# A gated recurrence over 512 steps: one VectorE transpose cut in two and two VectorE instructions moved to other places of the step

## The chip, the cores and the metric

The kernel runs on one core of one Trainium2 chip. The metric is the time of one execution in device microseconds. Three runs of the kernel before gave 1627.81, 1628.59 and 1628.85 us, a median of 1628.59 us.

## What is computed

The input `x` has 8 sequences of 512 steps with 512 features. A recurrent cell runs over the steps, and its states are added to `x`.

```
def step(h, x_t):                                   # h: 8 x 512, x_t: 8 x 512
    fused = sigmoid(concat([x_t, h]) @ w_W + w_b)   # 8 x 1024
    hidden_state, output_state = split(fused, 2)    # r and z below
    memory_state = x_t @ wx_W + wx_b + hidden_state * (h @ wh_W + wh_b)
    h_new = output_state * h + (1 - output_state) * tanh(memory_state)
    return h_new, h_new
_, hs = scan(step, cond_1024, x over its steps)
result = x + hs
```

The products with `x_t` can be made ahead of time. The products with `h` can't: each step needs the state of the step before, in all 512 features.

## The kernel before

**Layout.** The 512 state features are cut into four chunks of 128. Chunks 0 and 1 are half A (`hf` = 0 in the code), chunks 2 and 3 are half B (`hf` = 1). A state tile `hT` holds 128 features on the partitions and the 8 sequences beside each other, for 4 steps; 8 such tiles are used in turn. Four column groups of TensorE (32 columns each) work side by side, so one product with a chunk of the state is four matmuls, and float32 makes two passes of each.

**TensorE, one step.** The string `ORDER` sets the order: A0 to A3, then D0 to D3, then H2 and H3. The letter is the PSUM bank that is added to, the digit is the chunk of the state that is the stationary operand. Bank A collects half A's inner product, z and r (and half B's part of the inner product from chunks 0 and 1), bank D half B's z and r, and bank H the rest of half B's inner product. A0 and A1 stream 256 columns, A2 and A3 192, D0 to D3 128, H2 and H3 64. Behind them come products for later `x`, which do not depend on the state (bank `xp`): three blocks of 96 columns in a step, four in one step of sixteen, none in the last steps.

**VectorE, one step.** Its program is in the order in which the Python code is written. Half A comes first: transposes out of bank A (`turn_r`, `turn_h(0)`, `turn_z`), two scans `memory(0, q)`, a transpose for half B out of bank A (`turn_part`), the transpose of half B's r out of bank D (`turn_r_b`), then the update scans. `memory(hf, q)` is a scan that forms the argument of the tanh for chunk `q` of a half (tile `m`); ScalarE takes the tanh and writes it into `hT`. `update(hf, q)` is a scan that forms the new state of that chunk from z (`hd0A` or `hd0B`), the tanh and the old state. `turn_h(1)` transposes half B's inner product ("hh") from bank H into `md1B`. `turn_sz` transposes half B's z, on which ScalarE has taken the sigmoid already (tile `sz`), into `hd0B`, in two pieces of 32 columns, one for each chunk.

**Waits inside VectorE.** A scan that reads what an earlier VectorE instruction wrote needs a wait on that instruction's end. The kernel puts a memset of one column of `idle` in front of the scan, and the memset carries the wait (`settle`, and the memset at the end of `turn_sz`). The second piece of z has no such memset of its own; `update(1, 1)` waits for it itself.

**Who waits for whom.** On TensorE the weight loads of A0, A1, A2 and A3 each wait for one of the four updates of the step before, in the order `update(0, 0)`, `update(0, 1)`, `update(1, 0)`, `update(1, 1)`. On ScalarE the order is: sigmoid of half A's r and z, tanh of half A's chunks, sigmoid of half B's r in two pieces (`md0B`), sigmoid of half B's z (`sz`), tanh of half B's chunks, two copies of the new state. Behind the updates VectorE does work that has no hurry: it adds up the `x` products (`drain`, L431), turns them for later steps (`turn_x`, L319), and in the first steps forms differences of weights (`inner_weight`, L338). GpSimd adds `x` to the state and works on later `x`.

**Lines.** L219 is every matmul, L285 every ScalarE function, L565 every scan, L592 `turn_h`, L600 and L632 the memsets that wait, L629 z's transposes.

Of the kernel before, what the change touches and what calls it, by code (L numbers as in the profile page):

```python
# [24 lines left out]
SYNC = mybir.DependencyInfo(mybir.DependencyClass.Sync, mybir.DependencyReason.DATA)  # L25
# [51 lines left out]
def tile_cond_rnn_residual(  # L77
# [38 lines left out]
    nc = tc.nc  # L116
# [29 lines left out]
    def x_of(c, k, t, n):  # L146

        e, t = divmod(t, TC // 2)
        if c == 0 and e == 0:
            first = head[:, 512 : 512 + NX].rearrange("p (k n) -> p k n", k=NQ)  # L150
            return first[:, k, t * B : (t + n) * B]
        return xins[c][:, e, k, t * B : (t + n) * B]
# [18 lines left out]
    def pair(n, name, rows, slots):  # L171

        return const.tile([P, 2, rows, slots], F32, name=name).rearrange("p c n s -> p n c s")
# [3 lines left out]
    NH = 2 * GS  # L177
# [4 lines left out]
    md1 = [[pair(n, f"md1{n}{i}", 32, m) for i in range(2)] for n, m in (("A", 2), ("B", 3))]  # L182
    hd0 = [[pair(n, f"hd0{n}{i}", m, 3) for i in range(2)] for n, m in (("A", B), ("B", 32))]
# [24 lines left out]
    def state(hf, i, slot=2):  # L208

        s = i % GS  # L210
        return hT[hf][i % NH][:, B * s : B * s + B, :, slot]
# [72 lines left out]
    def act(key, out_, in_, func, **kw):  # L284
        inst = nc.scalar.activation(out_, in_, func, **kw).ins  # L285
        if key in written:
            tc.declare_no_dep(inst, written[key], reason="ordered through VectorE")
        written[key] = inst
        return inst

    def seed(g):

        at = COLS if g else slice(0, 512)
        nc.scalar.copy(bank_of(g)[:, at], bias[:, at])
# [228 lines left out]
    pool_done = {}  # L523
    for i in range(T):
        g, s = divmod(i, GS)
        c, t = divmod(i, TC)
# [36 lines left out]
        def scan(c_, out_, d0, d1):  # L563

            return nc.vector.tensor_tensor_scan(  # L565
                *[t_[:, :, c_].rearrange("p n c s -> p (n c s)") for t_ in (out_, d0, d1)],
                0.0,
                ALU.mult,
                ALU.add,
            ).ins  # L570

        pa = ps["A"][:, HU:] if i else xps[0][:, :HALF]
        raw = {"h": (pa[:, :HU], ps["H"]), "z": (pa[:, HU : 2 * HU],), "r": (pa[:, 2 * HU :], ps["D"][:, HU:])}
# [6 lines left out]
        h_done = [None, None]  # L580
# [8 lines left out]
            )  # L589

        def turn_h(hf):
            inst = nc.vector.transpose(  # L592
                md1[hf][g % 2][:, :, :, hf].rearrange("p n c -> p c n"), raw["h"][hf]
            ).ins
            h_done[hf] = inst
            if hf == 0 and i + 1 - NH in pool_done:
                tc.add_manual_dep(inst, pool_done[i + 1 - NH].name, SYNC)

        def settle(hf):
            inst = nc.vector.memset(idle[:, IDLE - 2 + hf : IDLE - 1 + hf], 0.0).ins  # L600
            tc.add_manual_dep(inst, h_done[hf].name, SYNC)
# [12 lines left out]
        def turn_r_b():  # L614
            t_, _ = turned("r", 1)
            for q in range(2):
                act(
                    ("r", 1, q, g % 2, s),
                    md0[1][g % 2][:, rows, q : q + 1, 2].rearrange("p n c -> p c n"),
                    t_[:, q : q + 1],  # L620
                    AF.Sigmoid,
                )
            sz = work.tile([P, HU], F32, tag="sz", name=f"sz_{i}")
            act(("sz", i % 4), sz, ps["D"][:, :HU], AF.Sigmoid, scale=-1.0)
            return sz

        def turn_sz(sz):
            done = [
                nc.vector.transpose(hd0[1][i % 2][:, :, q, 2], sz[:, 32 * q : 32 * q + 32]).ins  # L629
                for q in range(2)  # L630
            ]
            mark = nc.vector.memset(idle[:, IDLE - 3 : IDLE - 2], 0.0).ins  # L632
            tc.add_manual_dep(mark, done[0].name, SYNC)

        def turn_part():
            nc.vector.transpose(md1[1][g % 2][:, :, :, 0].rearrange("p n c -> p c n"), ps["A"][:, :HU])  # L636
# [6 lines left out]
        def memory(hf, q):  # L643

            c_ = slice(q, q + 1)
            scan(c_, ms[hf], md0[hf][g % 2][:, rows], md1[hf][g % 2][:, rows])
            act(("n", hf, q, i % NH), state(hf, i, 1)[:, :, c_], ms[hf][:, :, c_, 1 + hf], AF.Tanh)

        def update(hf, q):
            new = hT[hf][(i + 1) % NH][:, B * s1 : B * s1 + B]  # L650
            z_ = hd0[hf][i % 2][:, rows] if hf else hd0[hf][i % 2]
            return scan(slice(q, q + 1), new, z_, hT[hf][i % NH][:, rows])

        turn_r()
        turn_h(0)
        turn_z()
        memory(0, 0)
# [6 lines left out]
        sz = turn_r_b()  # L664
        update(0, 0)
        turn_h(1)
        update(0, 1)
        settle(1)
        if i == 0:

            seed(6)
        memory(1, 0)
        if i == T - 1:
            nc.gpsimd.tensor_tensor(
                ot[:, t, :2, :].rearrange("p c n -> p n c"),
                x_of(c, slice(0, 2), t, 1).rearrange("p c n -> p n c"),
                state(0, T),
                ALU.add,
            )
        memory(1, 1)  # L680
        turn_sz(sz)
        update(1, 0)
        update(1, 1)
        for hf in range(2):
            act(("h", hf, (i + 1) % NH), state(hf, i + 1, 0), state(hf, i + 1), AF.Copy)
# [129 lines left out]
```

## Time and profile before

| what | before |
|---|---|
| median of 3 runs | 1628.59 us (1627.81 to 1628.85) |
| profiled execution, first to last instruction | 1625.9 us |
| TensorE matmul busy | 1616.3 us (99%) |
| TensorE weight loads busy | 1308.3 us (80%) |
| VectorE busy | 1411.1 us (87%), 11757 instructions |
| ScalarE busy | 1023.8 us (63%) |
| GpSimd busy | 539.1 us (33%) |
| granted TensorE clock | 1.000 |

The span of the profiled execution is 2.7 us below the median of the timed runs; the rest is what lies around the first and the last instruction. In the profile, PE is the matmul stream of TensorE and PEld its weight loads, DVE is VectorE, ACT ScalarE, POOL GpSimd. The ends of matmuls are modelled, so a busy PE is not yet a PE that loses no time; the place to look is a wait of its weight loads, and the distance between the starts of the groups. With 512 steps in the span, 1 ns in each step is half a microsecond of the whole.

### The profile page before, as it was taken

The numbers are of one execution on the slowest core, as the hardware profiler recorded it, in microseconds if no ns is written. First come the engines' busy times: TensorE is split into PE (matmuls) and PEld (weight loads), VectorE is DVE, ScalarE is ACT, GpSimd is POOL, SyncE is SP. The second block draws the span as 40 slices with busy tenths as digits, with TensorE's granted clock in tenths as the row PEclk, the third lists the DMA queues.
The fourth block names the chain that finished last, engine by engine and source line by source line (L and its number), as shares of the span: only waits on it lengthen the run. The fifth ranks groups of instructions, "written<-read, shape, count | busy, mean of one in ns | idle before, by whom it ended". The sixth has DMA issues, their size and how long they took to land.

```text
span 1625.9 us, 120027 instructions
## 1 busy us (share of the span) xinstructions
PE 1616.3 (99%) x49211; PEld 1308.3 (80%) x49211; DVE 1411.1 (87%) x11757; ACT 1023.8 (63%) x6033; POOL 539.1 (33%) x1443
## 2 busy tenths in 40 slices
PE   9999999999999999999999999999999999999998
PEld 5888888888888888888888888888888888888876
DVE  8988888888888888888888888888888888888887
ACT  4666666666666666666666666666666666666665
POOL 2323333333333333333333333333333333333321
PEclk9999999999999999999999999999999999999999
DMA  4011111111111111111111111111111111110110
GB/s 192 12 40 33 29 37 38 43 32 33 31 43 39 35 34 31 39 38 39 33 29 37 38 43 32 30 35 43 38 33 34 32 39 38 39 34 25 31 35 10
DMA packets 66217, 62.04 MB, mean 38 GB/s; under 512 B 9856, under 2 KB 64000, under 8 KB 65664
## 3 DMA queue, kind: packets, MB, share of 16 engines
q1 hardware_dynamic: 65664, 54.35, 12.7%
q8 instruction: 385, 6.31, 1.7%
q14 instruction: 168, 1.38, 0.3%
HBM read 14.96 MB, written 8.39 MB: 14 GB/s over the span
## 4 chain that ended last, share of the span: by engine, by line
PE 98%; DVE 1%; issue 0%; ACT 0%; DVEq 0%
PE A L219 49%; PE D L219 27%; PE xp L219 16%; PE H L219 7%; DVE tr L577 0%; DVE m L565 0%; DVE md1B L636 0%; DVE hT L565 0%; DVE md1A L592 0%; DVE tz L577 0%; DVE zeros L185 0%; DVE hd0B L629 0%; DVE md1B L592 0%; DVE idle L600 0%; ACT hT L285 0%
## 5 line engine op out<-in xcount | busy, mean ns | idle before, releaser
L219 PE MATMUL A<-wa,hT 128*32 128x256 f32 x16352 | 877.8, 355 | 4.2 <-DVE hT L565 4.2
L219 PEld LDWEIGHTS A<-wa,hT 128*32 128x32 f32 x16352 | 497.5, 123 | 260.2 <-DVE hT L565 135.6
L219 PE MATMUL D<-wd,hT 128*32 128x128 f32 x16384 | 541.0, 273 | 0.0
L219 PEld LDWEIGHTS D<-wd,hT 128*32 128x32 f32 x16384 | 480.4, 122 | 21.8 <-DMA wd<-in_wd_dram 0.5
L731 POOL TENSOR_TENSOR ot<-xin,hT 128x32 f32<-128x32 f32 x503 | 134.4, 267 | 1046.5 <-DVE hT L565 1028.8
L285 ACT ACTIVATE md0A<-tr 128x16 f32<-128x16 f32 x512 | 112.9, 221 | 385.2 <-DVE tr L577 385.2
L285 ACT ACTIVATE hT<-m 128x8 f32<-128x8 f32 x2048 | 324.2, 207 | 46.8 <-DVE m L565 0.4
L577 DVE STREAM_TRANSPOSE tr<-A 128x64 f32<-128x64 f32 x511 | 127.8, 250 | 199.4 <-PE A L219 198.2
L285 ACT ACTIVATE hT<-hT 128x16 f32<-128x16 f32 x1024 | 232.3, 227 | 91.4 <-DVE hT L565 89.9
L219 PE MATMUL H<-wa,hT 128*32 128x64 f32 x8208 | 208.3, 219 | 0.0
L285 ACT ACTIVATE md0B<-tr 128x8 f32<-128x8 f32 x1024 | 160.0, 206 | 42.6 <-DVE tr L577 1.2
L219 PEld LDWEIGHTS H<-wa,hT 128*32 128x32 f32 x8208 | 185.6, 122 | 0.0
L565 DVE TENSOR_TENSOR_SCAN hT<-hd0B,hT 128x24 f32<-128x24 f32 x1024 | 171.4, 208 | 0.8 <-DVE hT L565 0.8
L565 DVE TENSOR_TENSOR_SCAN hT<-hd0A,hT 128x24 f32<-128x24 f32 x1024 | 171.9, 168 | 0.0
L565 DVE TENSOR_TENSOR_SCAN m<-md0B,md1B 128x24 f32<-128x24 f32 x1024 | 154.5, 193 | 0.5 <-issue 0.4
L629 DVE STREAM_TRANSPOSE hd0B<-sz 128x32 f32<-128x32 f32 x1024 | 148.5, 190 | 0.0
L565 DVE TENSOR_TENSOR_SCAN m<-md0A,md1A 128x16 f32<-128x16 f32 x1024 | 142.5, 181 | 5.1
L219 PE MATMUL xp<-ti,si 128*32 128x192 f32 (+1 forms) x3120 | 146.7, 295 | 0.0
L450 POOL TENSOR_TENSOR xs<-ff 128x192 f32<-128x192 f32 x240 | 139.5, 597 | 0.1
L636 DVE STREAM_TRANSPOSE md1B<-A 128x64 f32<-128x64 f32 x511 | 130.1, 255 | 0.0
L285 ACT ACTIVATE hd0A<-tz 128x16 f32<-128x16 f32 x512 | 116.6, 228 | 21.2
L592 DVE STREAM_TRANSPOSE md1B<-H 128x64 f32<-128x64 f32 x512 | 128.3, 251 | 0.0
(110 smaller groups left out, 1861.0 us busy)
## 6 DMA issues: line engine op xcount, KB each, us to landing
ff<-tt SPq DMA_DIRECT2D x120, 96.0 KB, 2.6
ff<-tt SPq DMA_DIRECT2D x120, 72.0 KB, 2.2
out_dram<-ot SPq DMA_DIRECT2D x128, 64.0 KB, 1.8
xin<-in_x_dram SPq DMA_DIRECT2D x112, 64.0 KB, 2.1
ff<-ff SPq DMA_DIRECT2D x60, 96.0 KB, 2.1
ff<-ff SPq DMA_DIRECT2D x60, 72.0 KB, 2.7
wx<-in_wx_dram SPq DMA_DIRECT2D x4, 768.0 KB, 7.3
wa<-in_wa_dram SPq DMA_DIRECT2D x4, 512.0 KB, 11.1
```

What stands on the lines that cost most here:

```text
L219: nc.tensor.matmul(out_, lhsT, rhs, start=start, stop=False, skip_group_check=True)
L285: inst = nc.scalar.activation(out_, in_, func, **kw).ins
L450: nc.gpsimd.tensor_tensor(to, a, b, ALU.add)
L565: return nc.vector.tensor_tensor_scan(*[t_[:, :, c_].rearrange("p n c s -> p (n c s)") for t_ in (out_, d0, d1)], 0.0, ALU.mult, ALU.add,).ins
L577: inst = nc.vector.transpose(t_.rearrange("p c n -> p (c n)"), raw[n][hf]).ins
L592: inst = nc.vector.transpose(md1[hf][g % 2][:, :, :, hf].rearrange("p n c -> p c n"), raw["h"][hf]).ins
L629: nc.vector.transpose(hd0[1][i % 2][:, :, q, 2], sz[:, 32 * q : 32 * q + 32]).ins
L636: nc.vector.transpose(md1[1][g % 2][:, :, :, 0].rearrange("p n c -> p c n"), ps["A"][:, :HU])
L731: pool_done[i + 1] = nc.gpsimd.tensor_tensor(ot[:, t], x_of(c, slice(0, NQ), t, 1), hTs[(i + 1) % NH][:, :, :, B * s1 : B * s1 + B, 2].rea ...
```

## The change

`turn_h(1)` becomes two transposes of 32 columns, one for each chunk of half B, and the memset of `settle(1)` waits for the first of them alone. `update(0, 1)` moves behind `memory(1, 0)`. z's first transpose moves in front of `memory(1, 1)`, z's second transpose behind `update(1, 0)`; the memset that waits for z's first transpose (now `settle_z`) stays in front of `update(1, 0)`.

```
         def turn_h(hf):
+            if hf:
+                for q in range(2):
+                    at = slice(32 * q, 32 * q + 32)
+                    inst = nc.vector.transpose(md1[1][g % 2][:, :, q, 1], raw["h"][1][:, at]).ins
+                    h_done[1] = h_done[1] or inst
+                return
             inst = nc.vector.transpose(
-                md1[hf][g % 2][:, :, :, hf].rearrange("p n c -> p c n"), raw["h"][hf]
+                md1[0][g % 2][:, :, :, 0].rearrange("p n c -> p c n"), raw["h"][0]
             ).ins
...
-        def turn_sz(sz):
-            done = [
-                nc.vector.transpose(hd0[1][i % 2][:, :, q, 2], sz[:, 32 * q : 32 * q + 32]).ins
-                for q in range(2)
-            ]
+        z_done = []
+
+        def turn_sz(sz, q):
+            z_done.append(nc.vector.transpose(hd0[1][i % 2][:, :, q, 2], sz[:, 32 * q : 32 * q + 32]).ins)
+
+        def settle_z():
             mark = nc.vector.memset(idle[:, IDLE - 3 : IDLE - 2], 0.0).ins
-            tc.add_manual_dep(mark, done[0].name, SYNC)
+            tc.add_manual_dep(mark, z_done[0].name, SYNC)
...
         update(0, 0)
         turn_h(1)
-        update(0, 1)
         settle(1)
...
         memory(1, 0)
+        update(0, 1)
...
+        turn_sz(sz, 0)
         memory(1, 1)
-        turn_sz(sz)
+        settle_z()
         update(1, 0)
+        turn_sz(sz, 1)
         update(1, 1)
```

What VectorE has in its program, in step 237, from `turn_r_b` to half B's first memory scan. A scan stands here as SCALAR_TENSOR_TENSOR; `hT6<-hd0A1` is an update of half A, `md1B1<-H1` is `turn_h(1)`, `m1_237` a memory scan of half B. Before:

```order
L577 STREAM_TRANSPOSE tr1_237_22457<-D1_173 128x64 [waits PE_49]
L565 SCALAR_TENSOR_TENSOR hT6_96<-hd0A1_107,hT5_95 128x24 [waits Activation_49]
L592 STREAM_TRANSPOSE md1B1_105<-H1_174 128x64 [waits PE_49]
L565 SCALAR_TENSOR_TENSOR hT6_96<-hd0A1_107,hT5_95 128x24 [waits Activation_49]
L600 MEMSET idle_148 128x1 [waits DVE_49]
```

The same place of the changed kernel:

```order
L577 STREAM_TRANSPOSE tr1_237_22694<-D1_173 128x64 [waits PE_49]
L565 SCALAR_TENSOR_TENSOR hT6_96<-hd0A1_107,hT5_95 128x24 [waits Activation_49]
L595 STREAM_TRANSPOSE md1B1_105<-H1_174 128x32 [waits PE_49]
L595 STREAM_TRANSPOSE md1B1_105<-H1_174 128x32
L606 MEMSET idle_148 128x1 [waits DVE_49]
```

The second update of half A no longer stands between the transpose of bank H and the memset, and the transpose is two instructions.

VectorE in the same step, from half B's first memory scan to its last update (`hd0B1<-sz` are z's transposes, `hT6<-hd0B1` the updates of half B). Before:

```order
L565 SCALAR_TENSOR_TENSOR m1_237_22443<-md0B1_101,md1B1_105 128x24 [waits Activation_49] x2
L629 STREAM_TRANSPOSE hd0B1_109<-sz_237_22461 128x32 [waits Activation_49]
L629 STREAM_TRANSPOSE hd0B1_109<-sz_237_22461 128x32
L632 MEMSET idle_148 128x1 [waits DVE_49]
L565 SCALAR_TENSOR_TENSOR hT6_96<-hd0B1_109,hT5_95 128x24 [waits Activation_49]
L565 SCALAR_TENSOR_TENSOR hT6_96<-hd0B1_109,hT5_95 128x24 [waits DVE_49,Activation_49]
```

The changed kernel:

```order
L565 SCALAR_TENSOR_TENSOR m1_237_22680<-md0B1_101,md1B1_105 128x24 [waits Activation_49]
L565 SCALAR_TENSOR_TENSOR hT6_96<-hd0A1_107,hT5_95 128x24
L636 STREAM_TRANSPOSE hd0B1_109<-sz_237_22698 128x32 [waits Activation_49]
L565 SCALAR_TENSOR_TENSOR m1_237_22680<-md0B1_101,md1B1_105 128x24 [waits DVE_49]
L639 MEMSET idle_148 128x1 [waits DVE_49]
L565 SCALAR_TENSOR_TENSOR hT6_96<-hd0B1_109,hT5_95 128x24 [waits Activation_49]
L636 STREAM_TRANSPOSE hd0B1_109<-sz_237_22698 128x32
L565 SCALAR_TENSOR_TENSOR hT6_96<-hd0B1_109,hT5_95 128x24 [waits DVE_49,Activation_49]
```

The second memory scan of half B has half A's second update and z's first transpose in front of it, and z's second transpose stands between the two updates of half B. TensorE, ScalarE, GpSimd and the DMA queues keep the instructions and the order that they had.

More of the change, by code (lines that the diff above doesn't have):

```diff
@@ L591, in turn_h @@
         def turn_h(hf):
+            if hf:
[4 more added lines that the diff above has]
+                return
             inst = nc.vector.transpose(
-                md1[hf][g % 2][:, :, :, hf].rearrange("p n c -> p c n"), raw["h"][hf]
+                md1[0][g % 2][:, :, :, 0].rearrange("p n c -> p c n"), raw["h"][0]
             ).ins
-            h_done[hf] = inst
-            if hf == 0 and i + 1 - NH in pool_done:
+            h_done[0] = inst
+            if i + 1 - NH in pool_done:
                 tc.add_manual_dep(inst, pool_done[i + 1 - NH].name, SYNC)
```

## The prediction

> **What bounds the kernel now.** I read the page first. It calls TensorE full, and the chain that ended last runs through it.
>
> ```profile
> span 1625.9 us, 120027 instructions
> PE 1616.3 (99%) x49211; PEld 1308.3 (80%) x49211; DVE 1411.1 (87%) x11757; ACT 1023.8 (63%) x6033; POOL 539.1 (33%) x1443
> PE 98%; DVE 1%; issue 0%; ACT 0%; DVEq 0%
> ```
>
> If that were all, reordering VectorE could change nothing. So I read the list of waits next: TensorE's weight loads of bank A wait for an update in nearly every step, 499 times, 0.27 us each.
>
> ```profile
> PEld A L219 <- DVE hT L565: 135.6, 499, 0.8
> ```
>
> A weight load may wait behind a running matmul without loss, so this row doesn't say what the wait costs. The timeline of one ordinary step does (columns: start in us, length in us, engine, line, operation, output and input). It reaches from one `tr<-A`, the transpose that opens VectorE's step, to the next.
>
> ```profile
> 807.69 0.25 DVE L577 STREAM_TRANSPOSE tr<-A 128x64 f32<-128x64 f32 x1 [0.25 <-PE A L219]
> ...
> 808.54 0.68 PE L219 MATMUL xp<-ti,si 128*32 128x96 f32 x16
> ...
> 808.74 0.17 DVE L565 TENSOR_TENSOR_SCAN hT<-hd0A,hT 128x24 f32<-128x24 f32 x1
> 808.83 0.25 DVE L592 STREAM_TRANSPOSE md1B<-H 128x64 f32<-128x64 f32 x1
> 808.85 0.31 ACT L285 ACTIVATE md0B<-tr 128x8 f32<-128x8 f32 x2
> ...
> 808.97 0.17 DVE L565 TENSOR_TENSOR_SCAN hT<-hd0A,hT 128x24 f32<-128x24 f32 x1
> 809.03 1.71 PE L219 MATMUL A<-wa,hT 128*32 128x256 f32 x32
> 809.06 0.20 ACT L285 ACTIVATE sz<-D 128x64 f32<-128x64 f32 x1
> 809.12 0.20 DVE L565 TENSOR_TENSOR_SCAN m<-md0B,md1B 128x24 f32<-128x24 f32 x1
> ...
> 809.24 0.18 DVE L565 TENSOR_TENSOR_SCAN m<-md0B,md1B 128x24 f32<-128x24 f32 x1
> 809.34 0.29 DVE L629 STREAM_TRANSPOSE hd0B<-sz 128x32 f32<-128x32 f32 x2
> 809.36 0.32 ACT L285 ACTIVATE hT<-m 128x8 f32<-128x8 f32 x2
> ...
> 809.60 0.21 DVE L565 TENSOR_TENSOR_SCAN hT<-hd0B,hT 128x24 f32<-128x24 f32 x1
> ...
> 809.73 0.21 DVE L565 TENSOR_TENSOR_SCAN hT<-hd0B,hT 128x24 f32<-128x24 f32 x1
> 809.86 0.53 DVE L431 TENSOR_TENSOR ff<-xp,ee 128x384 f32<-128x384 f32 x1
> 809.87 0.51 PEld L219 LDWEIGHTS A<-wa,hT 128*32 128x32 f32 x16 [0.26 <-DVE hT L565]
> ...
> 810.39 0.96 PEld L219 LDWEIGHTS D<-wd,hT 128*32 128x32 f32 x32
> ...
> 810.81 0.25 DVE L577 STREAM_TRANSPOSE tr<-A 128x64 f32<-128x64 f32 x1 [0.28 <-PE A L219]
> ```
>
> The step takes 3.12 us. The load at 809.87 is A2's; it begins 0.06 behind the end of `update(1, 0)` (809.60 + 0.21 = 809.81). Narrow windows of the same timeline show the starts inside bank A: A1's matmuls, A2's matmuls, A3's loads.
>
> ```profile
> 809.46 0.62 PE L219 MATMUL A<-wa,hT 128*32 128x256 f32 x8
> 809.89 0.68 PE L219 MATMUL A<-wa,hT 128*32 128x192 f32 x12
> 810.07 0.30 PEld L219 LDWEIGHTS A<-wa,hT 128*32 128x32 f32 x8
> ```
>
> Loads go one matmul group ahead, and a chunk is two groups. From A3's loads (810.07) to D's (810.39) are two groups, so 0.16 each. From A2's late load (809.87) to A3's it is 0.20: a load that comes late takes 0.04 more than a group, its group starts in effect at 809.91, and its place was 809.89. So TensorE loses 0.02 us in a step, and A1's place is 809.46.
>
> Two other stretches confirm that. In one step of sixteen there is a fourth block of `xp`:
>
> ```profile
> 817.04 0.25 DVE L577 STREAM_TRANSPOSE tr<-A 128x64 f32<-128x64 f32 x1 [0.47 <-PE A L219]
> 817.89 0.51 PE L219 MATMUL xp<-ti,xin 128*32 128x192 f32 x8
> ...
> 818.54 1.70 PE L219 MATMUL A<-wa,hT 128*32 128x256 f32 x32
> 820.30 0.25 DVE L577 STREAM_TRANSPOSE tr<-A 128x64 f32<-128x64 f32 x1 [0.39 <-PE A L219]
> ```
>
> There `xp` takes 0.65 (817.89 to 818.54) instead of 0.49 (808.54 to 809.03), 0.16 more, and the step 3.26, only 0.14 more. TensorE's own work is therefore 3.10 in an ordinary step. And near the end, where there is no `xp` at all, the step is still 3.11:
>
> ```profile
> 1599.27 0.25 DVE L577 STREAM_TRANSPOSE tr<-A 128x64 f32<-128x64 f32 x1 [0.85 <-PE A L219]
> 1602.38 0.25 DVE L577 STREAM_TRANSPOSE tr<-A 128x64 f32<-128x64 f32 x1 [0.85 <-PE A L219]
> ```
>
> So the step is a loop: `tr<-A`, 2.18 us to A2's load, 0.20 + 0.32 to D's load, 0.41 to the next `tr<-A`. TensorE's own 3.10 stands just below it. A change can win 0.02 a step at most, and can lose any amount.
>
> **The change, followed through the same step.** `update(0, 0)` stays at 808.74. The first half of bank H's transpose starts at 808.83. The trace has 32-column transposes out of PSUM only at the start (`md1B<-xp`); for z's I take the view of tile `hd0B` (shortest, median, longest in ns).
>
> ```profile
> 15.88 0.28 DVE L319 STREAM_TRANSPOSE md1B<-xp 128x32 f32<-128x32 f32 x2
> L629 DVE STREAM_TRANSPOSE hd0B<-sz x1024: 175/189/229, 23.1 to 1622.8; 128x32 f32<-128x32 f32 x171
> L285 ACT ACTIVATE hT<-m 128x8 f32<-128x8 f32 x2048 | 324.2, 207 | 46.8 <-DVE m L565 0.4
> L285 ACT ACTIVATE md0B<-tr 128x8 f32<-128x8 f32 x1024 | 160.0, 206 | 42.6 <-DVE tr L577 1.2
> ```
>
> The first half ends at 809.02, both at 809.11 (a pair takes 0.28). Today `memory(1, 0)` starts 0.04 behind the end of the whole transpose (808.83 + 0.25 = 809.08, then 809.12). With the wait on the first half that alone would give 809.06. But the scan also needs the first sigmoid, 808.85 + 0.21 = 809.06, and VectorE starts 0.03 behind a ScalarE end (the first tanh ends at 809.36 + 0.21 = 809.57, `update(1, 0)` starts at 809.60). So `memory(1, 0)` starts at 809.09, 0.03 earlier. The extra instruction costs nothing, covered by that sigmoid.
>
> `update(0, 1)` follows 0.12 later (the distance of the two memory scans), from 809.21 to 809.38, and A1's load can start at 809.44. Counted with the 0.04 its group starts at 809.48, 0.02 behind its place: the loss that A2 has today turns up at A1. z's first transpose starts 0.09 behind that scan (808.74 to 808.83), at 809.30, just when `sz` is there (809.06 + 0.20 + 0.03 = 809.29), and ends at 809.49. `memory(1, 1)` comes to 809.41 or so and ends at 809.59; its tanh ends near 809.83.
>
> `update(1, 0)` still waits for the first tanh, so it inherits the 0.03 and no more: 809.57. A2's load at 809.84 (809.57 + 0.21 + 0.06) is then in time.
>
> Now the new wait. z's second transpose stands behind `update(1, 0)`, and `update(1, 1)` reads what it writes. Today that transpose ends at 809.63 (809.34 + 0.29) and `update(1, 1)` starts at 809.73, 0.10 behind: a wait for the end and not for a free engine, although the transpose was started long before. In the changed kernel the price is exposed: 0.13 from `update(1, 0)` to the transpose (as from 809.73 to the next VectorE instruction at 809.86), 0.19 for the transpose, 0.10 for the wait, 0.42 in all where today it is 0.13. `update(1, 1)` starts at 809.57 + 0.42 = 809.99 and ends at 810.20; A3's load starts at 810.26. Its place is 810.07, with room up to 810.19 (A2's effective start of 809.91, 0.32 for A2's groups, less 0.04). It is 0.07 late. D's load comes 0.20 behind it, at 810.46 instead of 810.39, and the next `tr<-A` at 810.88. The loop is now 2.57 to A3's load + 0.20 + 0.41 = 3.18 to 3.19 instead of 3.12: **0.07 us longer in an ordinary step**. A1's 0.02 lies inside it.
>
> Queued behind the waiting `update(1, 1)` on VectorE are `drain`, `turn_x` and the rest; they have 0.25 us or more before the next `tr<-A` in ordinary steps (its row says 0.28 at 810.81) and 0.07 more is added, so a shift of 0.26 fits. GpSimd's add and ScalarE's copy wait for `update(1, 1)` too, and have room: GpSimd is 33% busy. In the first steps VectorE has no room:
>
> ```profile
> 59.80 0.07 DVE L710 MEMSET idle<- 128x1 f32 x2
> 59.83 0.25 DVE L577 STREAM_TRANSPOSE tr<-A 128x64 f32<-128x64 f32 x1
> ```
>
> There `tr<-A` follows the last weight difference at once. The code spreads these over 16 steps. Each loses between 0 and 0.26; I take 0.15.
>
> The sum: of 512 steps 36 have a fourth block and its 3.26 us, which covers 3.19, so nothing is lost; 16 are the early ones; 460 remain. 460 x 0.07 = 32.2, 16 x 0.15 = 2.4, and 0.2 for the last update, which the last store waits for: 34.8 us. The profiled execution would have a span of 1660.7; the runs' median lies 2.7 above the span, and comes to 1663.4.
>
> Unknown are the transpose's start and length. If it starts 0.10 behind the scan (809.24 to 809.34 today) and takes 0.18, the loss is 0.03 a step: 13.8 + 1.8 + 0.2, so 1644. I keep 0.13, since there the instruction ahead is the same scan. If the first half brings `memory(1, 0)` nothing, the loss is 0.10: 46 + 2.9 + 0.2, so 1678. There is no gain to bound beyond TensorE's 0.02.
>
> **Rivals.** *The wait is free.* The Trainium skill, "VectorE: DVE Perf Modes", section "The DRAIN you can't avoid", says that the next VectorE instruction starts only when the pipe is empty, and that a semaphore after each then costs nothing extra. As a mechanism here: `update(1, 1)` would start where the transpose ends, at 809.89, and A3's load at 810.16, inside its room. Then only A1's 0.02 is left in place of A2's, and the time stays at 1629. Against it stands the 0.10 behind the transpose's end, which the skill's rule doesn't have; and 809.73 lies before 809.81, the end of the scan ahead. Chance 0.06.
>
> *TensorE alone bounds.* The wait is free and `update(0, 1)` follows 0.10 behind the memory scan, as z's transpose does today. A1's load is then in time, each step takes 3.10, and 476 x 0.02 = 9.5 us go: 1619. This is the case on the faster side. It turns if `update(1, 1)` starts before 809.92 and `update(0, 1)` before 809.19. Chance 0.06.
>
> *The memset waits for both halves.* The order shows a wait on VectorE, not on which instruction. Then `memory(1, 0)` starts at 809.11 + 0.04 = 809.15, 0.06 behind my 809.09, the step loses 0.13: 460 x 0.13 + 16 x 0.21 + 0.2 = 63.4, and 1692. Chance 0.07.
>
> **How the numbers follow.** The forecast, 1663.4 with 1644 to 1678 as its own range, has 0.81. That range leaves out the three rivals, 0.19 together, so it stands as the range of the whole. About 0.2% is what a measurement of this kernel can tell from no change. Faster 0.06 (TensorE alone), same 0.06 (free wait), slower 0.88 (0.81 + 0.07).
>
> **What would show it.** Right: in an ordinary step z's second transpose starts some 0.13 behind `update(1, 0)`, `update(1, 1)` 0.10 behind the transpose's end, and the weight loads of A wait for `hT` at A3, not at A2; steps of 3.19 us, and 3.26 still where there is a fourth block. `memory(1, 0)` starts 0.03 earlier against `tr<-A`. Wrong: `update(1, 1)` right at the transpose's end, A3's loads at their place, or steps of 3.12 or less.

## The result, and the profile after

The changed kernel takes 1683.0 us (median of 5 runs, 1682.66 to 1683.34), the kernel before 1628.59 us beside it (5 runs, 1627.81 to 1628.85). The ratio is 1.0335 (95% interval 1.0322 to 1.0347): 54.4 us slower. The prediction said 1663.4, with a range up to 1678; the sign and the place were right, the size was not.

The page of the changed kernel, span, busy time and the chain of work that ended last:

```profile
span 1680.9 us, 120539 instructions
PE 1669.5 (99%) x49211; PEld 1231.0 (73%) x49211; DVE 1514.7 (90%) x12269; ACT 1083.9 (64%) x6033; POOL 539.8 (32%) x1443
PE 78%; DVE 2%; issue 0%; ACT 0%; DVEq 0%
```

TensorE still reads 99% busy, with the same 49211 matmuls: its busy time grew by 53 us, nearly the whole loss. The ends of matmuls are modelled in the profile, so this share tells nothing of where the time went. The list of waits does (engine, line, who is waited for: us in all, times, longest):

```profile
PEld A L219 <- DVE hT L565: 368.1, 1594, 0.8
DVE tr L577 <- PE A L219: 84.7, 313, 0.7
```

The loads of bank A waited 499 times before, about once a step; now 1594 times, about three times a step. Which of the three matters is seen in the timeline of an ordinary step (start, length, engine, line, operation):

```profile
828.65 0.25 DVE L577 STREAM_TRANSPOSE tr<-A 128x64 f32<-128x64 f32 x1 [0.30 <-PE A L219]
...
829.78 0.30 DVE L595 STREAM_TRANSPOSE md1B<-H 128x32 f32<-128x32 f32 x2
...
830.06 0.21 DVE L565 TENSOR_TENSOR_SCAN m<-md0B,md1B 128x24 f32<-128x24 f32 x1
830.18 0.18 DVE L565 TENSOR_TENSOR_SCAN hT<-hd0A,hT 128x24 f32<-128x24 f32 x1
...
830.42 0.19 PEld L219 LDWEIGHTS A<-wa,hT 128*32 128x32 f32 x8 [0.29 <-DVE hT L565]
830.55 0.21 DVE L565 TENSOR_TENSOR_SCAN hT<-hd0B,hT 128x24 f32<-128x24 f32 x1
830.67 0.20 DVE L636 STREAM_TRANSPOSE hd0B<-sz 128x32 f32<-128x32 f32 x1
830.81 0.23 PEld L219 LDWEIGHTS A<-wa,hT 128*32 128x32 f32 x8 [0.20 <-DVE hT L565]
830.98 0.21 DVE L565 TENSOR_TENSOR_SCAN hT<-hd0B,hT 128x24 f32<-128x24 f32 x1
...
831.24 0.19 PEld L219 LDWEIGHTS A<-wa,hT 128*32 128x32 f32 x8 [0.20 <-DVE hT L565]
831.44 0.96 PEld L219 LDWEIGHTS D<-wd,hT 128*32 128x32 f32 x32
831.85 0.25 DVE L577 STREAM_TRANSPOSE tr<-A 128x64 f32<-128x64 f32 x1
```

A1's load (830.42), A2's (830.81) and A3's (831.24) each come behind an update. Only the last one sets the end: D's load stands 0.20 behind A3's in every ordinary step (0.32 before, where A3's load was in time), and the next `tr<-A` 0.41 behind D's. A3's load waits for `update(1, 1)` (830.98), which waits for z's second transpose (830.67 + 0.20 = 830.87). The step takes 3.20 us, where it was 3.12.

Some steps lose more. Here is one of them with GpSimd's work, first a step of that kind before:

```profile
863.37 1.15 POOL L450 TENSOR_TENSOR ff<-ff 128x192 f32<-128x192 f32 x2
...
863.94 0.25 DVE L577 STREAM_TRANSPOSE tr<-A 128x64 f32<-128x64 f32 x1 [0.50 <-PE A L219]
...
864.47 0.28 DVE L565 TENSOR_TENSOR_SCAN m<-md0A,md1A 128x16 f32<-128x16 f32 x2
```

and one of the changed kernel:

```profile
851.20 1.15 POOL L450 TENSOR_TENSOR xs<-ff 128x192 f32<-128x192 f32 x2
...
851.57 0.25 DVE L577 STREAM_TRANSPOSE tr<-A 128x64 f32<-128x64 f32 x1 [0.36 <-PE A L219]
...
852.10 0.38 DVE L565 TENSOR_TENSOR_SCAN m<-md0A,md1A 128x16 f32<-128x16 f32 x2
...
854.84 0.25 DVE L577 STREAM_TRANSPOSE tr<-A 128x64 f32<-128x64 f32 x1 [0.20 <-PE A L219]
```

The row of GpSimd is two additions that follow `update(1, 1)`. Before, they end at 864.52, 0.05 behind the start of half A's memory scans in the next step, and the two scans take 0.28. Now they end at 852.35, 0.25 behind it, and the scans take 0.38; this step takes 3.27. The groups of instructions show that over the whole span, before and then after (busy us, mean ns, idle before):

```profile
L565 DVE TENSOR_TENSOR_SCAN m<-md0A,md1A 128x16 f32<-128x16 f32 x1024 | 142.5, 181 | 5.1
```

```profile
L565 DVE TENSOR_TENSOR_SCAN m<-md0A,md1A 128x16 f32<-128x16 f32 x1024 | 161.2, 198 | 5.3
```

No instruction of this group was edited or moved, and it takes 18.7 us longer.

Put step against step over the two traces, the 55.0 us of span are: 460 ordinary steps with 0.086 each, 39.6 us; in 149 of these a long memory scan of half A with another 0.075 each, 11.2 us; 31 steps with a fourth block with 0.042 each, 1.3 us; the first 17 steps, 2.1 us; some 0.8 in what is left.

### The profile page after: what moved, and what is told of

Same layout as the page of the kernel before. It is cut to its first block, busy times and chain, and to the rows that moved or that the text cites. A ratio compares the mean times of both kernels' runs of the same rounds, so it can differ in the third digit from the quotient of the medians.

```text
span 1680.9 us, 120539 instructions
## 1 busy us (share of the span) xinstructions
PE 1669.5 (99%) x49211; PEld 1231.0 (73%) x49211; DVE 1514.7 (90%) x12269; ACT 1083.9 (64%) x6033; POOL 539.8 (32%) x1443
## 3 DMA queue, kind: packets, MB, share of 16 engines
q1 hardware_dynamic: 65664, 54.35, 12.3%
## 4 chain that ended last, share of the span: by engine, by line
PE 78%; DVE 2%; issue 0%; ACT 0%; DVEq 0%
PE A L219 40%; PE D L219 20%; PE xp L219 12%; PE H L219 5%; DVE tr L577 0%; DVE m L565 0%; DVE hT L565 0%; DVE md1B L643 0%; DVE md1A L598 0%; DVE tz L577 0%; ACT hT L285 0%; DVE md1B L595 0%; DVE hd0B L636 0%; DVE idle L606 0%; DVE idle L719 0%
## 5 line engine op out<-in xcount | busy, mean ns | idle before, releaser
L219 PE MATMUL A<-wa,hT 128*32 128x256 f32 x16352 | 923.9, 363 | 5.6 <-DVE hT L565 5.4
L219 PEld LDWEIGHTS A<-wa,hT 128*32 128x32 f32 x16352 | 415.4, 125 | 395.5 <-DVE hT L565 368.1
L285 ACT ACTIVATE hT<-m 128x8 f32<-128x8 f32 x2048 | 381.9, 211 | 94.1 <-DVE m L565 0.6
L565 DVE TENSOR_TENSOR_SCAN hT<-hd0B,hT 128x24 f32<-128x24 f32 x1024 | 212.7, 208 | 54.5 <-ACT hT L285 1.4
L636 DVE STREAM_TRANSPOSE hd0B<-sz 128x32 f32<-128x32 f32 x1024 | 206.6, 202 | 0.0
L565 DVE TENSOR_TENSOR_SCAN m<-md0B,md1B 128x24 f32<-128x24 f32 x1024 | 190.4, 186 | 0.4 <-ACT sz L285 0.4
L565 DVE TENSOR_TENSOR_SCAN hT<-hd0A,hT 128x24 f32<-128x24 f32 x1024 | 185.5, 181 | 0.0
L565 DVE TENSOR_TENSOR_SCAN m<-md0A,md1A 128x16 f32<-128x16 f32 x1024 | 161.2, 198 | 5.3
L595 DVE STREAM_TRANSPOSE md1B<-H 128x32 f32<-128x32 f32 x1024 | 154.4, 195 | 0.0
```

Of the source, the lines that this page charges most:

```text
L219: nc.tensor.matmul(out_, lhsT, rhs, start=start, stop=False, skip_group_check=True)
L565: return nc.vector.tensor_tensor_scan(*[t_[:, :, c_].rearrange("p n c s -> p (n c s)") for t_ in (out_, d0, d1)], 0.0, ALU.mult, ALU.add,).ins
L595: inst = nc.vector.transpose(md1[1][g % 2][:, :, q, 1], raw["h"][1][:, at]).ins
L636: z_done.append(nc.vector.transpose(hd0[1][i % 2][:, :, q, 2], sz[:, 32 * q : 32 * q + 32]).ins)
```

## The experiments

The theories that the runs test: **W**: the loss is `update(1, 1)`'s wait for z's second transpose, which makes A3's load late. **R1**, the rival to it: the loss is `update(0, 1)` behind `memory(1, 0)`, which makes A1's load late. **G**: on top of either, GpSimd's additions, released later by `update(1, 1)`, hold half A's next memory scan; its rival **G'** is that any late GpSimd instruction does so, whatever it reads. Each time stands beside that of the kernel before on the same chip, and two kernels are compared by their losses against it.

### z's second transpose back in front of the update (z_back)

Against the changed kernel:

```
+        turn_sz(sz, 1)
         settle_z()
         update(1, 0)
-        turn_sz(sz, 1)
         update(1, 1)
```

> The changed kernel with one part undone: z's second transpose stands in front of update(1, 0) again, the rest as changed. Theory W (the new wait of update(1, 1) behind z's second transpose is what each step pays, 0.086 us): update(1, 1) no longer waits 0.10 behind a transpose that has only just started, but update(1, 0) has one more instruction in front of it and starts 0.06 to 0.10 later than in the changed kernel; A2 becomes the late load; steps of 3.16 to 3.20 instead of 3.20, and no long memory scan of half A, since GpSimd's work shifts by less: 1648 to 1669 us. Rival R1 (what is paid is update(0, 1) in its new place, A1's load): A1's load stays where it is, the steps stay at 3.20, 1670 us or more.

Measured: 1640.36 us, before 1628.01, ratio 1.0076 (1.0061 to 1.0091). The loss is 12.3 us, so 42 of the 54.4 us hang on the place of this one instruction, and R1 falls as the main cause: `update(0, 1)` stands behind `memory(1, 0)` here too. The time lies below W's range too: `update(1, 0)`, with the transpose ahead of it, came at 1.94 us into the step where W had 1.96 to 2.00. In the timeline of z_back A1's and A2's loads come late, and A3's follows in the same row as A2's:

```profile
840.38 0.25 DVE L577 STREAM_TRANSPOSE tr<-A 128x64 f32<-128x64 f32 x1
...
842.16 0.19 PEld L219 LDWEIGHTS A<-wa,hT 128*32 128x32 f32 x8 [0.28 <-DVE hT L565]
842.59 0.51 PEld L219 LDWEIGHTS A<-wa,hT 128*32 128x32 f32 x16 [0.24 <-DVE hT L565]
```

### The wait taken away, the order kept (no_raw)

Against the changed kernel; half B's second update reads the other z buffer, so it does not wait for z's second transpose:

```
-            z_ = hd0[hf][i % 2][:, rows] if hf else hd0[hf][i % 2]
+            z_ = hd0[hf][(i + q) % 2][:, rows] if hf else hd0[hf][i % 2]
```

> The changed kernel with the same instructions in the same order, but update(1, 1) reads z from the other buffer of the pair (the step before's), so that it no longer has to wait for z's second transpose. The states of chunk 3 are wrong therefore. Theory W (the wait on that transpose is what a step pays): update(1, 1) starts when its tanh is there, about 2.19 us behind the step's first transpose instead of 2.33; A3's load is in time; what is left is A1's load, late by 0.04 behind update(0, 1): steps of 3.14, no scan over 0.24 us, 1638 to 1643. Rival R3 (the place of the transpose costs by itself, the engine being full, and not the wait): steps stay near 3.20, 1670 or more.

Measured: 1637.71 us, before 1627.17, ratio 1.0067 (1.0052 to 1.0082), 0.3 below W's range and far from R3's. The same instructions in the same order:

```profile
841.12 0.25 DVE L577 STREAM_TRANSPOSE tr<-A 128x64 f32<-128x64 f32 x1 [0.16 <-PE A L219]
...
842.88 0.19 PEld L219 LDWEIGHTS A<-wa,hT 128*32 128x32 f32 x8 [0.27 <-DVE hT L565]
...
843.14 0.20 DVE L636 STREAM_TRANSPOSE hd0B<-sz 128x32 f32<-128x32 f32 x1
843.28 0.55 PEld L219 LDWEIGHTS A<-wa,hT 128*32 128x32 f32 x16 [0.20 <-DVE hT L565]
843.31 0.21 DVE L565 TENSOR_TENSOR_SCAN hT<-hd0B,hT 128x24 f32<-128x24 f32 x1
```

`update(1, 1)` starts at 843.31, before the transpose ends (843.14 + 0.20 = 843.34), and A3's load is in time: it follows in A2's row, and D's load stands 0.28 behind it in the median, no longer 0.20. The loss is 10.5 us, so the wait, with what it brings about, is 43.9 of the 54.4. Without it an ordinary step still loses 0.020; A1's late load (842.88, 1.76 into the step) is then no longer hidden behind A3's. I did not take that away alone.

### Half the columns of GpSimd's second addition (gp_short)

Against the changed kernel; the second addition of a step is given `w` = `HALF // 2`, the first stays whole:

```
-    def result(e, n):
+    def result(e, n, w=HALF):
...
-        nc.gpsimd.tensor_tensor(to, a, b, ALU.add)
+        nc.gpsimd.tensor_tensor(to[:, :w], a[:, :w], b[:, :w], ALU.add)
```

> The changed kernel, with half of the columns left out of the second GpSimd addition (L450) of each step that has two, so that GpSimd is done before half A's first memory scan. Those x products are wrong therefore; no other engine's work is changed. Theory G (the first memory scan of half A takes 0.29 instead of 0.19 us in 180 steps because GpSimd's addition still runs): all scans at 0.19, the 149 ordinary steps that took 3.28 take 3.20, and 12 to 13 us go: 1670 to 1672. Rival R2 (the long scan comes from ScalarE or from a DMA that moved): the scans stay long, 1683.

Measured: 1671.27 us, before 1628.01, ratio 1.0265 (1.025 to 1.028). The loss is 43.3 us; the 11.1 less than the changed kernel's are G's, and the scans are short again. In the timeline the two additions end at 853.31, 0.04 behind the scan's start:

```profile
852.37 0.94 POOL L450 TENSOR_TENSOR ff<-ff 128x192 f32<-128x192 f32 x2
...
853.27 0.28 DVE L565 TENSOR_TENSOR_SCAN m<-md0A,md1A 128x16 f32<-128x16 f32 x2
```

### A memset of the same length instead of the addition (gp_memset)

Against the changed kernel; `pad` has 608 columns:

```
+            if m and job is result:
+                nc.gpsimd.memset(pad, 0.0)
+            else:
+                job(*args)
```

> The changed kernel with the second GpSimd addition of each step that has two left out (those x products are wrong therefore) and in its place a memset of 608 columns, which lasts about as long and reads nothing. Theory G, with the port that the two engines share for reads as the reason: half A's first memory scan stays at 0.19 although GpSimd is busy beside it, 1670 to 1672. Theory G', any GpSimd instruction stops the scan: scans of 0.29, 1683.

Measured: 1669.48 us, before 1627.17, ratio 1.026 (1.0243 to 1.0277), a loss of 42.3 us, about that of gp_short. In the timeline:

```profile
851.87 0.60 POOL L749 MEMSET pad<- 128x608 f32 x1
...
852.24 0.28 DVE L566 TENSOR_TENSOR_SCAN m<-md0A,md1A 128x16 f32<-128x16 f32 x2
```

GpSimd is busy until 852.47, 0.23 behind the scan's start, as late as in the changed kernel, and the scans take 0.28. G' falls: an addition, which reads, holds the scan, and a memset, which only writes, does not.

### GpSimd later in the kernel before (gp_late, gp_late2)

Against the kernel before, one memset of 64 columns ahead of the additions, and then two:

```
+        if any(job is result for job, *_ in jobs.get(i, ())):
+            nc.gpsimd.memset(pad, 0.0)
```

> The kernel before with one more GpSimd instruction, a memset of 64 columns (about 0.23 us) ahead of the additions (L450) of a step. VectorE, ScalarE and TensorE have the same program. Theory G: GpSimd's second addition now ends 0.27 instead of 0.045 us behind the start of half A's first memory scan, the scan takes 0.3 instead of 0.19 us in about 180 steps, and about 150 ordinary steps are 0.075 us longer: 1638 to 1642. Rival R2: no scan gets longer, 1629.

Measured for one memset: 1627.64 us, before 1628.01, ratio 0.9998 (0.9989 to 1.0007). A miss, and not yet a verdict: the memset takes 0.151 us, but moved the additions by only 0.085. They ended 0.13 behind the scan's start, and the scans did not get longer:

```profile
866.77 1.15 POOL L451 TENSOR_TENSOR xs<-ff 128x192 f32<-128x192 f32 x2
...
867.79 0.28 DVE L566 TENSOR_TENSOR_SCAN m<-md0A,md1A 128x16 f32<-128x16 f32 x2
```

> The kernel before with two GpSimd memsets of 64 columns ahead of the additions of a step (one memset moved the additions by 0.085 us). VectorE, ScalarE and TensorE have the same program. Theory G: the second addition ends 0.23 us behind the start of half A's first memory scan, and the scan ends 0.047 behind it, 0.28 long instead of 0.19; some 149 ordinary steps are 0.06 to 0.075 longer and 31 with a fourth block 0.02 to 0.03: 1637 to 1640. Rival R2 (long scans come from something else that moves with update(1, 1)): scans of 0.19, 1628.

Measured for two: 1637.86 us, before 1627.17, ratio 1.0068 (1.0053 to 1.0083). In the timeline the additions end at 841.81, 0.22 behind the scan's start, and the scans take 0.35 instead of 0.28:

```profile
840.65 1.16 POOL L451 TENSOR_TENSOR xs<-ff 128x192 f32<-128x192 f32 x2
...
841.59 0.35 DVE L566 TENSOR_TENSOR_SCAN m<-md0A,md1A 128x16 f32<-128x16 f32 x2
```

The 149 ordinary steps with such an addition took 0.074 us more each, 11.0 us; the others did not change. So GpSimd's lateness alone makes this loss, with VectorE's and TensorE's programs as they were.

### The three parts alone (split_only, move_only, z_only)

Each against the kernel before: only the two transposes of 32 columns; only `update(0, 1)` moved; only z's second transpose moved.

```
+                for q in range(2):
+                    at = slice(32 * q, 32 * q + 32)
+                    inst = nc.vector.transpose(md1[1][g % 2][:, :, q, 1], raw["h"][1][:, at]).ins
```

> The kernel before with one part of the change alone: the transpose of bank H for half B as two of 32 columns, the memset behind it waiting for the first. Theory (VectorE is full between the transpose of bank H and update(1, 0), so one more instruction there is paid where no wait covers it): update(0, 1) stands behind two transposes, 0.08 later, memory(1, 0) follows at 1.455 instead of 1.428 behind the step's first transpose and update(1, 0) with it: steps of 3.145, 1639 to 1643. Rival (the second transpose hides behind the sigmoid as in the changed kernel): 1628 or less.

```
-        update(0, 1)
         settle(1)
...
         memory(1, 0)
+        update(0, 1)
```

> The kernel before with one part of the change alone: update(0, 1) behind memory(1, 0). The whole transpose of bank H still sets memory(1, 0), 1.428; update(0, 1) follows at 1.55 and A1's load is late by 0.06; z's transposes come 0.11 to 0.12 later and update(1, 0) starts near 1.97 instead of 1.913, A2's load late by 0.08: steps of 3.16 to 3.18, no long scan, 1648 to 1660. Rival (update(0, 1) has the room that the prediction of the change gave it, 0.02): 1637 or less.

```
-            done = [
-                nc.vector.transpose(hd0[1][i % 2][:, :, q, 2], sz[:, 32 * q : 32 * q + 32]).ins
-                for q in range(2)
-            ]
+            done = nc.vector.transpose(hd0[1][i % 2][:, :, 0, 2], sz[:, :32]).ins
...
         update(1, 0)
+        nc.vector.transpose(hd0[1][i % 2][:, :, 1, 2], sz[:, 32:64])
         update(1, 1)
```

> The kernel before with one part of the change alone: z's second transpose behind update(1, 0). Theory W: update(1, 0) stays 1.91 us behind the step's first transpose, then 0.125 to the transpose, 0.20 for it, 0.10 for the wait: update(1, 1) at 2.34 instead of 2.04, steps of 3.22 instead of 3.12, 47 us; with 2 to 3 us of the early steps and, by theory G, 11 to 13 us of long scans, 1688 to 1692. Without G 1677. Rival R1: update(0, 1) is where it was, nothing is paid, 1629.

| kernel | measured | before | ratio (95%) | ordinary step, mean |
|---|---|---|---|---|
| split_only | 1634.35 | 1626.75 | 1.0047 (1.0033 to 1.0061) | +0.014 us |
| move_only | 1660.22 | 1626.75 | 1.0206 (1.0192 to 1.022) | +0.067 us |
| z_only | 1696.12 | 1628.01 | 1.0418 (1.04 to 1.0435) | +0.103 us, +0.199 with a long scan |

None of the three lies inside its expected range. split_only falls between its theory and its rival; move_only is 0.2 above its theory's; z_only is 4 above, because a long scan costs an ordinary step another 0.096 there, and the steps with a fourth block lose some 0.07 as well. The rivals of move_only (1637 or less) and of z_only (nothing is paid) fall.

Alone they lose 7.6, 33.5 and 68.1 us, 109 together, where the whole change loses 54.4. The timeline of move_only shows why:

```profile
840.97 0.20 DVE L565 TENSOR_TENSOR_SCAN m<-md0B,md1B 128x24 f32<-128x24 f32 x1
...
841.09 0.18 DVE L565 TENSOR_TENSOR_SCAN hT<-hd0A,hT 128x24 f32<-128x24 f32 x1
841.19 0.18 DVE L565 TENSOR_TENSOR_SCAN m<-md0B,md1B 128x24 f32<-128x24 f32 x1
841.29 0.29 DVE L629 STREAM_TRANSPOSE hd0B<-sz 128x32 f32<-128x32 f32 x2
841.54 0.20 DVE L565 TENSOR_TENSOR_SCAN hT<-hd0B,hT 128x24 f32<-128x24 f32 x1
```

VectorE is full from half B's first memory scan to `update(1, 0)`. The update moved into that stretch takes 0.12 of it, and `update(1, 0)` comes at 841.54, 0.57 behind the scan instead of 0.48 (809.12 to 809.60 before). In the whole change z's second transpose leaves that stretch and makes the room; the price is the wait behind it. Beside z_only, the other two parts give 13.7 us back.

### Two versions meant to do better (regroup, regroup_gp)

The order is `turn_h(1)`'s first half, `update(0, 1)`, memset, `memory(1, 0)`, second half, z in one transpose of 64 columns, `memory(1, 1)`, memset, both updates. The second version also spreads GpSimd's additions over more steps:

```
-            return nc.vector.transpose(hd0[1][i % 2][:, :, q, 2], sz[:, 32 * q : 32 * q + 32]).ins
+            return nc.vector.transpose(hd0[1][i % 2][:, :, :, 2].rearrange("p n c -> p c n"), sz).ins
...
-        for e, w, jobs_ in ((0, 13, ((0, 3), (2, 4), (1,), (5, 6))), (1, 18, ((0, 3), (1, 2), (4, 5), (6,)))):
+        for e, w, jobs_ in ((0, 13, ((0, 3), (2, 4), (1,), (5,), (6,))), (1, 18, ((0,), (3,), (2,), (4,), (1,), (5,), (6,)))):
```

> A version that takes the readings together: first half of bank H's transpose, update(0, 1), memset, memory(1, 0), second half, z's transpose in one of 64 columns, memory(1, 1), memset, the two updates of half B. One instruction fewer than the changed kernel, no wait on a transpose that has just started, update(0, 1) where it was. By the starts and lengths of the runs so far update(1, 0) comes at 1.90 (1.913 before), update(1, 1) at 2.23 behind its tanh, just in time: steps of 3.105 to 3.115. But update(1, 1) is later by 0.19 than before, so GpSimd's second addition ends some 0.2 behind the start of half A's first memory scan, and about 149 steps pay 0.04 to 0.07: 1624 to 1634.

> The version before this one, with GpSimd's additions spread so that of eight steps in sixteen with additions two instead of six have two of them. Theory G: only some 60 long scans instead of 180 are left, and the gain of the steps remains: 1621 to 1628. If the long scans had another reason, as the version before this one.

Measured: regroup 1647.34 us, ratio 1.0126 (1.0112 to 1.014); regroup_gp 1654.06, ratio 1.0168 (1.0154 to 1.0182); before 1626.75. Both missed. In the timeline of regroup:

```profile
839.87 0.25 DVE L577 STREAM_TRANSPOSE tr<-A 128x64 f32<-128x64 f32 x1 [0.18 <-PE A L219]
...
841.70 0.21 DVE L565 TENSOR_TENSOR_SCAN m<-md0B,md1B 128x24 f32<-128x24 f32 x1
...
841.94 0.21 ACT L285 ACTIVATE hT<-m 128x8 f32<-128x8 f32 x1 [0.15 <-DVE idle L636]
...
842.19 0.21 DVE L565 TENSOR_TENSOR_SCAN hT<-hd0B,hT 128x24 f32<-128x24 f32 x1
...
842.45 0.19 PEld L219 LDWEIGHTS A<-wa,hT 128*32 128x32 f32 x8 [0.16 <-DVE hT L565]
```

`memory(1, 1)` comes late behind the 64-column transpose, its tanh with it (841.94 to 842.15), and A3's load is late again; now that tanh is what `update(1, 1)` waits for. About half of regroup's loss is G's all the same: the ordinary steps with a long scan take another 0.07, some 10 us. In regroup_gp the first scan is long in 57 ordinary steps instead of 149. But some moved additions stand in steps in which GpSimd has other work, which then ends later still, and in 56 more steps the second scan is held by that work:

```profile
854.97 0.60 POOL L450 TENSOR_TENSOR ff<-ff 128x192 f32<-128x192 f32 x1
855.52 0.46 POOL L353 TENSOR_TENSOR so<-so,xin 128x128 f32<-128x128 f32 x1
...
855.87 0.59 DVE L565 TENSOR_TENSOR_SCAN m<-md0A,md1A 128x16 f32<-128x16 f32 x2
...
855.95 0.46 POOL L353 TENSOR_TENSOR so<-xin 128x128 f32<-128x128 f32 x1
```

The two scans take 0.59 there and end 0.05 behind GpSimd (855.95 + 0.46 = 856.41). The held steps cost 0.15 each, some 17 us in all, and the 6.7 us between the two versions are that. No version beat the kernel before.

## Why the prediction was right, and where it was wrong

The path on VectorE and TensorE was right, step by step, and the price of GpSimd was missing. Times in us from the step's first transpose, medians over the ordinary steps except where one step is named:

| | predicted | measured |
|---|---|---|
| `memory(1, 0)` | 1.40 | 1.405 |
| A1's load | 1.75 | 1.77 (the step shown) |
| `update(1, 0)` | 1.88 | 1.897 |
| z's second transpose, its length | 2.01, 0.19 | 2.022, 0.200 |
| `update(1, 1)` behind the transpose's end | 0.10 | 0.103 |
| `update(1, 1)` | 2.30 | 2.325 |
| A3's load | 2.57 | 2.59 (the step shown) |
| the step | 3.18 to 3.19 | 3.20 |

**Mis-sized: "0.07 us longer in an ordinary step".** It was 0.086 without the collision, 39.6 us instead of 32.2. `update(1, 0)` did not inherit the whole 0.03 of `memory(1, 0)`: the scan came 0.023 earlier, the update 0.016. With the transpose 0.01 longer, `update(1, 1)` came 0.025 late against the forecast. Rows rounded to 0.01 can carry that much error when five of them are added. This term is 7.4 us of the 19.6 that the forecast fell short.

**Failed: "GpSimd's add and ScalarE's copy wait for `update(1, 1)` too, and have room: GpSimd is 33% busy".** The share of busy time was the wrong evidence. GpSimd is idle for two thirds of the time, but its additions start behind `update(1, 1)`, and in the kernel before they already ended 0.05 behind the start of the next memory scan. The prediction followed who waits for `update(1, 1)` by semaphores, not who reads the same memory beside them, and it put the term at nothing. The lateness costs 11.2 us in the ordinary steps by the step comparison, 11.1 by gp_short, and 11.0 us for the 149 ordinary steps when it is brought about alone (gp_late2).

The Trainium skill, "SBUF — State Buffer", section "Who interferes with whom", has this rule: a VectorE instruction with two inputs in SBUF contends with a GpSimd instruction that reads SBUF, not with one that only writes it. gp_short, gp_memset and gp_late2 agree with it; the scans have two inputs (`md0A,md1A`). The section also calls the ports that the two engines share an exclusive lock. The runs show less than that for a short overlap: with the addition's end up to 0.13 us behind the scan's recorded start, the scan lost nothing.

**Smaller terms.** The first steps lost 2.1 us, where the sum had 2.4 for 16 of them. Six of the 36 steps with a fourth block (`PLAIN` in the kernel) lie among these 16, so the sum counted them twice and left out six ordinary steps, 0.4 us. The steps with a fourth block were to lose nothing; 31 of them have a long scan as well and lose 0.042, 1.3 us together. "A1's 0.02 lies inside it" fits the step shown: A1's load is late, and D's load follows A3's all the same. The sign that the loads of A would wait "at A3, not at A2" was not met as written: A1's and A2's rows have a wait too, but they do not set the end.

**The rivals.** *The wait is free* fell: `update(1, 1)` starts 0.103 behind the transpose's end in the median, and taking the wait away gives 43.9 us back. The Trainium skill's rule that the prediction weighed ("VectorE: DVE Perf Modes", section "The DRAIN you can't avoid"), in which a semaphore behind each VectorE instruction costs nothing extra, doesn't hold for this pair: without the wait `update(1, 1)` started as early as 0.17 behind the start of the transpose (843.14 to 843.31), with it 0.31 (830.67 to 830.98). *TensorE alone bounds* needed the same free wait. *The memset waits for both halves* fell: `memory(1, 0)` starts at 830.06, while the pair of transposes ends at 830.08.

Without the collision the changed kernel takes 1671.27 us (gp_short), inside the forecast's range of 1644 to 1678 and 8 above its 1663.4. The collision carried it past the upper end.

## What to carry to other kernels

Where an instruction is released later, follow what it does next on its own engine into the following step, and ask which instruction of another engine reads the same memory then; a share of 33% says nothing about that moment. A wait on the engine's own last instruction can hide behind what stands between the two; here the transpose moved next to the scan that needs it exposed the wait in every turn of the loop. The prices of parts tried alone need not add up when they fill or empty the same stretch: here 109 us alone, 54 us together.

## What the runs showed of the hardware that I had not expected

A scan of VectorE with two inputs is held by an addition of GpSimd only beyond a margin. With the addition's end 0.05 (before) or 0.13 us (gp_late) behind the scan's recorded start, the scan kept its 0.19 us. With 0.21 to 0.26 (gp_late2, the changed kernel) it ended about 0.047 behind the addition's end. z_back and no_raw lie between and fit: with 0.16 to 0.20 the scan took 0.21 to 0.24, again until 0.047 behind the addition. Over the scans that met an addition in the nine traces with these additions, the length is the longer of 0.192 and the addition's lateness plus 0.047, and the margin is the difference of the two, 0.145. A memset of GpSimd that ended 0.23 to 0.25 behind the start (gp_memset) cost the scan nothing. VectorE's transposes out of PSUM beside the same additions were no longer than without them: those of bank A into `md1A` took 0.21 us on average either way (the kernel before and gp_late2).

A memset of 64 columns on GpSimd takes 0.151 us by its row and moved the next instruction by only 0.085.
